# PSUM banks in a delta-rule attention: two for the pair steps, one for quantization and modulation

## The chip, the cores and the metric

The kernel runs on one core of a Trainium2 chip. Five engines work side by side, each through its own instructions in order: TensorE (PE, matmuls; its weight loads are listed as PEld), VectorE (DVE), ScalarE (ACT), GpSimd (POOL) and SyncE (SP, which here only issues DMAs). Matmul results land in PSUM, which has eight banks; ACT and DVE read them from there. The metric is the time of one execution on the device in microseconds (us), as the median of several runs.

## The reference

Two transformer blocks run one after the other on x of 2 batches, 1024 tokens and 512 channels. Each computes `x + ga * attn(norm(x) * (1 + ca) + sa)`, then the same with a feed-forward part and `sb, cb, gb`. The six vectors come from `silu(c) @ wmod`; this is called modulation. The two gates are kept away from zero: their magnitude is at least 0.25.

The attention of layer 0 is a gated delta rule with a state H of 64 x 64 per batch:

```
pred = q H;  surprise = sigmoid(sum((v - pred)^2))
H = a * H + (1 - a) * surprise * k^T (v - k H)
y = q H
```

k and q are normalized projections of the 512 channels to 64, v is a third projection and the decay a comes from a fourth through a sigmoid. y is normalized and projected back to 512.

The feed-forward part of layer 0 uses ternary weights. Each group of 64 weights has the mean of its magnitudes as a scale, and every weight becomes -1, 0 or 1 times that scale. The kernel does this quantization on the chip. Layer 1 has an RWKV attention and a feed-forward part with integer weights; the change doesn't touch it.

## The kernel before, in words

Tokens go in 16 chunks of 64 per batch, with both batches on the 128 partitions. Two chunks make a group, so that there are eight groups in layer 0's attention. For each group there are four kinds of work.

- `project(g)` normalizes two chunks, transposes them (`pt_a`), projects them (`pk`, `pv`) and leaves the scaled k and q in `kqr` (L385, L386).
- `pairs(g)` prepares all that doesn't need the state: products of each pair of steps in a chunk. It forms `kl` on DVE (L396), takes `pd` on PE, then six levels `pg` with decays multiplied in on DVE between them, then `pe`, `pm2`, `pse`, `pki` and `pik`, each a few small matmuls that are copied out by DVE or ACT before the next one. The last copy is `ik` (L475).
- `delta_chunk(c)` carries the state through one chunk. Its first DVE step is `wa` (L544), the new state is `h` (L518). It writes to the pool `ps_u`.
- `attention_out(g)` normalizes and projects y (`poa`) and adds it to x (`res_a` L229 on DVE, `xs` L230 on POOL).

Beside these, two other jobs fill the engines. `modulation(n)` loads a 512 x 512 slice of `wmod`, forms a row in `ps_...` (16 matmuls), copies it to `mrow_...` (L154, ACT), and turns it into columns (`pc_...`, read by DVE at L165) or a gate (`pg_ga`, `pg_gb`, read by ACT at L174 and by DVE at L176). `quantize(4)` calls `ternary` for four blocks of 128 x 512 weights: two ACT passes (`q_ab` L659, `q_sg` L661), one matmul that sums magnitudes (`pm_gu` L663), a copy out (`q_sc` L665, ACT), five DVE operations (L669 to L674) and a cast into the weight tile `wgu` (L675, ACT). There are 32 such blocks. The SBUF tiles of a block rotate through two buffers each.

`scan_all` writes the order of the program text. For g = 0 to 7: the two chunks of group g, `pairs(g + 2)`, `project(g + 3)`, `attention_out(g)`, one or two slices of modulation, and `quantize(4)`. (In the first round `pairs(1)` and `pairs(2)` both come here.) The text isn't the order on the engines. When the kernel is built, a planner puts the instructions of each engine in an order, from what it reckons to be ready and with work that stands earlier in the text first; it also hands out the buffers of each pool and adds the waits. That order is then fixed.

PSUM in layer 0's attention is dealt out by pools of whole banks: `ps_p` two (projection), `ps_g` one (pair steps), `ps_q` two (modulation and quantization), `ps_u` two (chunks) and `ps_o` one (output), eight in all. All tiles with the same tag share the buffers of that tag, and a tile gets a buffer when the earlier tile in it has been read for the last time. All names of `pairs` carry the tag `pg`. The pools are closed after the last group (`sp.close()`), and the feed-forward part opens `misc` (four banks, used first by the transposes `pt_f`, L202) and its own `ps_o` (four banks) in their place. Its SBUF tiles, `hh` and `hl` first, likewise take the place of the attention's; `good` (L712) is the last reduction of the attention.

The program holds the whole computation a second time with a step-by-step recurrence, behind a condition that is false for these inputs. The change edits its code too, but it isn't executed.

Of the kernel before, what the change touches and what calls it, by code (L numbers as in the profile page):

```python
# [8 lines left out]
F32 = mybir.dt.float32  # L9
# [5 lines left out]
PSUM = bass.MemoryType.PSUM  # L15

P = 128
B, S, D = 2, 1024, 512
ND = D // P
TT = 64  # L20

NC = S // TT
GT = 2
# [19 lines left out]
def block_pair_kernel(ctx: ExitStack, tc: tile.TileContext, a: dict, out: bass.AP):  # L43
    nc = tc.nc

    def pool(stack, name, bufs=1, **kw):
        return stack.enter_context(tc.tile_pool(name=name, bufs=bufs, **kw))
# [66 lines left out]
    def run(general, rs):  # L114
# [136 lines left out]
        with ExitStack() as la:  # L251
# [5 lines left out]
            sp = ExitStack()  # L257
# [1 line left out]

            ps_p = pool(sp, "ps_p", bufs=2, space=PSUM)  # L260
            ps_g = pool(sp, "ps_g", bufs=1, space=PSUM)
            ps_q = pool(sp, "ps_q", bufs=2, space=PSUM)
            ps_u = pool(sp, "ps_u", bufs=2, space=PSUM)
            ps_o = pool(sp, "ps_o", bufs=1, space=PSUM)
            proj = work = pool(sp, "proj", bufs=1)
# [35 lines left out]
            def both(to, weights, moving, start=True, stop=True, **kw):  # L301

                for b in range(B):
                    rows = slice(b * DS, (b + 1) * DS)
                    nc.tensor.matmul(  # L305
                        to[rows], weights[rows], moving[rows], start=start, stop=stop, **kw
                    )
# [81 lines left out]
            def pairs(g, kqr, al, v):  # L389

                gm = gms[g % 3]
                kqv = kqr.rearrange("p i (j t) -> p i j t", j=GT)
                gmv = gm.rearrange("p (j i) t -> p j i t", j=GT)
                kl = pair.tile([P, GT, TT], F32, tag="kl", name=f"kl_{g}", bufs=2)
                klf = kl.rearrange("p j t -> p (j t)")
                nc.vector.scalar_tensor_tensor(  # L396
                    klf, al, 1.0, kqr[:, 0], ALU.subtract, ALU.mult
                )

                pd = ps_g.tile([P, GT, TT], F32, tag="pg", name=f"pd_{g}")  # L400
                for j in range(GT):
                    both(pd[:, j], kl[:, j], kqv[:, 1, j])
                nc.vector.copy_predicated(
                    gmv[:, :, 2, :], mdiag.unsqueeze(1).to_broadcast([P, GT, TT]), pd
                )

                tot = al
                for h in LEVELS:  # L410
                    nb = TT // (2 * h)
                    ps = ps_g.tile([P, GT, 3, TT // 2], F32, tag="pg", name=f"pg_{g}_{h}")
                    right = kqr.rearrange("p i (n two h) -> p i n two h", two=2, h=h)[:, :, :, 1, :]
                    for j in range(GT):
                        both(
                            ps[:, j].rearrange("p i (n h) -> p i n h", h=h), kl[:, j],
                            right[:, :, j * nb:(j + 1) * nb, :],
                        )
                    nc.vector.copy_predicated(
                        gm.rearrange("p i (n two h) -> p i n two h", two=2, h=h)[:, :, :, 1, :],  # L420
                        masks[h].rearrange("p (n h) -> p n h", h=h).unsqueeze(1).to_broadcast(
                            [P, GT * 3, nb, h]
                        ),
                        ps.rearrange("p j i (n h) -> p (j i) n h", h=h),
                    )
                    tv = tot.rearrange("p (n two) -> p n two", two=2)
                    left = klf.rearrange("p (n two h) -> p n two h", two=2, h=h)[:, :, 0, :]
                    nc.vector.tensor_tensor(
                        left, left, tv[:, :, 1].unsqueeze(2).to_broadcast([P, GT * nb, h]), ALU.mult
                    )  # L430
                    nc.vector.tensor_tensor(
                        right, right,
                        tv[:, :, 0].unsqueeze(1).unsqueeze(3).to_broadcast([P, 3, GT * nb, h]),
                        ALU.mult,
                    )
                    nxt = pair.tile([P, GT * nb], F32, tag=f"tot{h}", name=f"tot_{g}_{h}")
                    nc.vector.tensor_tensor(nxt, tv[:, :, 0], tv[:, :, 1], ALU.mult)
                    tot = nxt
                atot = scan.tile([P, GT], F32, tag="atot", name=f"atot_{g}", bufs=3)
                nc.vector.tensor_copy(atot, tot)  # L440
                pe = ps_g.tile([P, GT, 3, TT], F32, tag="pg", name=f"pe_{g}")
                for j in range(GT):
                    both(pe[:, j, 0], kl[:, j], eye)
                    both(pe[:, j, 1], gmv[:, j, 0], eye)
                    both(pe[:, j, 2], kqv[:, 0, j], eye)

                kem = scan.tile([P, GT, 3, TT], F32, tag="kem", name=f"kem_{g}", bufs=3)
                nc.scalar.copy(kem, pe)

                im = pair.tile([P, GT, TT], F32, tag="im", name=f"im_{g}")  # L450
                nc.gpsimd.tensor_tensor(
                    im, gmv[:, :, 0], eye.unsqueeze(1).to_broadcast([P, GT, TT]), ALU.add
                )
                pm2 = ps_g.tile([P, GT, TT], F32, tag="pg", name=f"pm2_{g}")
                for j in range(GT):
                    both(pm2[:, j], gmv[:, j, 0], kem[:, j, 1])
                m2 = pair.tile([P, GT, TT], F32, tag="m2", name=f"m2_{g}")
                nc.scalar.copy(m2, pm2)
                pse = ps_g.tile([P, GT, TT], F32, tag="pg", name=f"pse_{g}")
                for j in range(GT):  # L460
                    both(pse[:, j], m2[:, j], im[:, j])
                inv = scan.tile([P, GT, TT], F32, tag="inv", name=f"inv_{g}", bufs=3)
                nc.vector.tensor_tensor(inv, pse, im, ALU.add)

                pki = ps_g.tile([P, GT, 2, TT], F32, tag="pg", name=f"pki_{g}")
                for j in range(GT):
                    both(pki[:, j, 0], kem[:, j, 2], inv[:, j])
                    both(pki[:, j, 1], inv[:, j], eye)
                ki = scan.tile([P, GT, 2, TT], F32, tag="ki", name=f"ki_{g}", bufs=3)
                nc.scalar.copy(ki, pki)  # L470
                pik = ps_g.tile([P, GT, TT], F32, tag="pg", name=f"pik_{g}")
                for j in range(GT):
                    both(pik[:, j], ki[:, j, 1], kem[:, j, 0])
                ik = scan.tile([P, GT, TT], F32, tag="ik", name=f"ik_{g}", bufs=3)
                nc.scalar.mul(ik, pik, 0.5)  # L475
                return gmv, kqv, kem, inv, atot, v, ki, ik
# [123 lines left out]
            def scan_all(chunk, p, name):  # L600
                h = p.tile([P, DS], F32, tag="h", name=f"h_init{name}")
                nc.vector.memset(h, 0.0)
                state[0] = h
                ops = [pairs(0, *project(0))]
                modulation(1)
                ahead = [project(1)]
                for g in range(NG):
                    yT = scan.tile([P, GT, TT], F32, tag="yT", name=f"yT_{g}{name}")
                    ysq = scan.tile([P, GT, TT], F32, tag="ysq", name=f"ysq_{g}{name}")
                    for j in range(GT):  # L610
                        chunk(GT * g + j, j, ops[g], yT, ysq)

                    for n in range(len(ops), min(g + 3, NG)):
                        ops.append(pairs(n, *ahead[n - 1]))
                        if n == g + 1:
                            attention_out(g, yT, ysq, f"{g}{name}")
                        for n in range(len(ahead) + 1, min(n + 2, NG)):
                            ahead.append(project(n))
                    if g:
                        attention_out(g, yT, ysq, f"{g}{name}")  # L620
                    modulation((1, 1, 1, 1, 1, 2, 1, 1)[g])
                    quantize(ND)
# [671 lines left out]
    with ExitStack() as rs:  # L1294
        bad = run(False, rs)
# [4 lines left out]
    with tc.If(odd != 0):  # L1300
        with ExitStack() as rs:
            run(True, rs)
# [46 lines left out]
```

## Time and profile before

| what | value |
|---|---|
| time, median of 3 runs | 1224.29 us (1224.22 to 1228.45) |
| the profiled execution: its time | 1233.09 us |
| its span, first to last instruction | 1231.2 us |
| granted TensorE clock, mean | 0.951 |
| PE busy | 1138.4 us (92%) |
| DVE busy | 730.3 us (59%) |
| ACT busy | 636.8 us (52%) |
| POOL busy | 410.4 us (33%) |

The profile is of one execution, so that its durations add up to its own span and not to the median. A row of the timeline gives the start in us from the start of the span, the duration in us, engine, line, operation, the tiles written and read, their shapes and the count; in brackets stands the idle time of the engine just before it and what ended that. Rows of the chain of work give start, duration and what ran. In the table of stretches each engine has its busy us and the number of its instructions; PEclk is the clock granted to TensorE. Matmuls are pipelined and their ends are modelled: a busy PE isn't PE at its peak.

### The profile page before, as it was taken

What the parts mean: (1) busy time and instruction counts of PE and PEld (TensorE: products, weight loads), DVE (VectorE), ACT (ScalarE), POOL (GpSimd) and SP (SyncE); (2) the same over time, 40 slices, a digit from 0 to 9 for tenths busy, and PEclk for the clock granted to TensorE, in tenths of its full rate; (3) what the DMA queues carried; (4) which work ended last, traced back from release to release, by engine and by line L of the source; (5) the groups of instructions that cost most, each with busy time, mean ns of one, the idle gap of its engine ahead of it and who ended that gap; (6) DMA issues with size and microseconds to landing.
All of it is one profiled execution on the core that took longest, in us unless ns stands there. A gap on an engine that the chain in (4) does not pass through costs nothing.

```text
span 1231.2 us, 17856 instructions
## 1 busy us (share of the span) xinstructions
PE 1138.4 (92%) x6746; PEld 854.5 (69%) x6746; DVE 730.3 (59%) x1509; ACT 636.8 (52%) x1423; POOL 410.4 (33%) x350
## 2 busy tenths in 40 slices
PE   5899999987999899999999979989899799999996
PEld 3667667554776688788788755737566488888884
DVE  3377677788777722622422789979899724242322
ACT  3367666567666533433433687876655644242421
POOL 1020112223444644644644313213212424242422
PEclk9899899876999999999999979979999899999998
DMA  8432121311110000000002311110000101010101
GB/s 204 113 87 71 35 89 62 127 54 35 52 43 26 1 1 1 1 1 1 1 35 69 95 35 35 52 35 1 1 1 10 43 26 35 1 35 1 35 1 38
DMA packets 40975, 48.72 MB, mean 40 GB/s; under 512 B 11568, under 2 KB 24880, under 8 KB 40880
## 3 DMA queue, kind: packets, MB, share of 16 engines
q1 hardware_dynamic: 39504, 45.92, 13.0%
q10 hardware_dynamic: 1376, 1.57, 0.4%
q8 instruction: 55, 0.90, 0.3%
q14 instruction: 40, 0.33, 0.1%
HBM read 43.28 MB, written 4.19 MB: 39 GB/s over the span
## 4 chain that ended last, share of the span: by engine, by line
PE 64%; DVE 21%; ACT 9%; issue 3%; POOL 2%; DMA 1%; SPq 1%; DVEq 0%; ACTq 0%
PE gu L762 14%; PE gui L1234 13%; PE pof L749 6%; PE poi L1214 6%; PE pow L1122 3%; PE pk L346 2%; PE pkvr L974 2%; DVE nd L1095 2%; PE u L305 2%; DVE q_m_p L671 2%; DVE xm L965 2%; PE pg L305 2%; PE poa L305 1%; PE pv L360 1%; DVE q_d_p L669 1%
## 5 line engine op out<-in xcount | busy, mean ns | idle before, releaser
L762 PE MATMUL gu<-hh,wgu 128*128 128x512 f32 x512 | 204.6, 402 | 4.9 <-DVE sg L771 3.5
L762 PE MATMUL gu<-hl,wgu 128*128 128x512 f32 x512 | 201.2, 395 | 4.0 <-DVE hl L221 2.7
L1234 PE MATMUL gui<-hp,wi 128*128 128x512 f32 x704 | 165.9, 390 | 0.0
L1234 PEld LDWEIGHTS gui<-hp,wi 128*128 128x128 f32 x704 | 131.8, 188 | 28.2 <-issue 0.8
L777 POOL TENSOR_TENSOR h0l<-sg,h0h 128x512 fp32r<-128x512 f32 x64 | 82.7, 1293 | 168.9 <-ACT h0h L775 168.9
L771 DVE TENSOR_TENSOR sg<-gu,sg 128x512 f32<-128x512 f32 x64 | 44.0, 687 | 139.9 <-ACT sg L770 136.6
L762 PEld LDWEIGHTS gu<-hh,wgu 128*128 128x128 f32 x512 | 97.3, 190 | 30.6 <-DVE sg L771 8.4
L762 PEld LDWEIGHTS gu<-hl,wgu 128*128 128x128 f32 x512 | 96.6, 189 | 27.1 <-DVE hl L221 4.5
L1249 POOL TENSOR_TENSOR h1l<-th,h1h 128x512 fp32r<-128x512 f32 x44 | 56.7, 1289 | 139.9 <-ACT h1h L1247 139.9
L1242 DVE SCALAR_TENSOR_TENSOR th<-th,gui 128x512 f32<-128x512 f32 x44 | 30.2, 687 | 121.7 <-ACT th L1241 121.7
L775 ACT CAST h0h<-sg 128x512 fp32r<-128x512 f32 x64 | 39.7, 621 | 86.8 <-DVE sg L773 84.9
L783 POOL TENSOR_TENSOR acc<-acc,hq 128x512 f32<-128x512 f32 x60 | 83.7, 1396 | 0.0
L1122 PE MATMUL pow<-w_wo,rw 128*64 128x512 f32 x256 | 73.5, 665 | 10.4 <-DVE rw L1113 10.0
L770 ACT ACTIVATE sg<-gu 128x512 f32<-128x512 f32 x64 | 38.1, 595 | 81.4 <-PE gu L762 81.4
L749 PE MATMUL pof<-wp,h0h 128*128 128x512 f32 x256 | 69.3, 392 | 1.7 <-ACT wp L675 1.7
L749 PE MATMUL pof<-wp,h0l 128*128 128x512 f32 x256 | 68.7, 389 | 0.0
L974 PE MATMUL pkvr<-xm,w_wk 128*128 128x256 f32 x256 | 62.1, 397 | 7.0 <-DVE xm L965 7.0
L1241 ACT ACTIVATE th<-gui,hsgate 128x512 f32<-128x512 f32 x44 | 30.3, 689 | 71.7 <-PE gui L1234 71.7
L1247 ACT CAST h1h<-th 128x512 fp32r<-128x512 f32 x44 | 27.3, 622 | 77.2 <-DVE th L1244 77.2
L974 PEld LDWEIGHTS pkvr<-xm,w_wk 128*128 128x128 f32 x256 | 48.3, 195 | 23.8 <-DVE xm L965 12.2
L974 PE MATMUL pkvr<-xm,w_wv 128*128 128x256 f32 x256 | 57.1, 380 | 1.0 <-DVE xm L965 1.0
L974 PE MATMUL pkvr<-xm,w_wr 128*128 128x256 f32 x256 | 56.6, 379 | 0.0
(368 smaller groups left out, 2497.6 us busy)
## 6 DMA issues: line engine op xcount, KB each, us to landing
wm<-in_wmod SPq DMA_DIRECT2D x22, 512.0 KB, 4.6
qst_gu<-in_wgu SPq DMA_DIRECT2D x32, 256.0 KB, 2.7
qst_p<-in_wp SPq DMA_DIRECT2D x16, 256.0 KB, 2.5
out<-oi SPq DMA_DIRECT2D x28, 128.0 KB, 2.4
xs<-in_x SPq DMA_DIRECT2D x2, 1536.0 KB, 15.8
kvt<-in_wq_gate SPq DMA_DIRECT2D x8, 256.0 KB, 2.6
kvt<-in_wq_up SPq DMA_DIRECT2D x8, 256.0 KB, 2.6
ist<-in_wq_down SPq DMA_DIRECT2D x7, 256.0 KB, 2.5
```

What stands on the lines that cost most here:

```text
L305: nc.tensor.matmul(to[rows], weights[rows], moving[rows], start=start, stop=stop, **kw)
L749: nc.tensor.matmul(pos[j], part[:, j * P:(j + 1) * P], wp[i // 4][:, i % 4, :], start=(i == 0 and z == 0), stop=(i == NH0 - 1 and z == 1),)
L762: nc.tensor.matmul(o, wgu[i // 4][:, d, s, (i % 4) * P:(i % 4 + 1) * P], part[:, d], start=(n == 0), stop=(n == 2 * ND - 1),)
L771: nc.vector.tensor_tensor(sg, gu[0], sg, ALU.mult)
L775: nc.scalar.copy(h1, h)
L777: nc.gpsimd.tensor_tensor(h2, h, h1.bitcast(F32), ALU.subtract)
L783: nc.gpsimd.tensor_tensor(acc, acc, hq, ALU.add)
L974: nc.tensor.matmul(ps[:, c * B:(c + 1) * B].rearrange("p b t -> p (b t)"), wkvr[i][:, d, (2 * z + c) * P:(2 * z + c + 1) * P], xm[d].rearr ...
L1122: nc.tensor.matmul(po[b * TT:(b + 1) * TT], rw[:, c, b, j * TT:(j + 1) * TT], wo1[:, c, :], start=(c == 0), stop=(c == ND - 1),)
L1214: nc.tensor.matmul(pos[j], part[:, j * P:(j + 1) * P], wdi[i // HS][:, i % HS, :], start=(i == 0 and z == 0), stop=(i == NH1 - 1 and z == ...
L1234: nc.tensor.matmul(o, wgi[i // HS][:, d, s, (i % HS) * P:(i % HS + 1) * P], part[:, d], start=(d == 0 and z == 0), stop=(d == ND - 1 and z ...
L1249: nc.gpsimd.tensor_tensor(h2, h, h1.bitcast(F32), ALU.subtract)
```

## The change

The pool `ps_q` gets one buffer in place of two, and the freed bank goes to `ps_g`: the tag of every PSUM tile in `pairs` becomes `pg0` for even groups and `pg1` for odd ones. The pool `ps_g` keeps `bufs=1`, now for two tags, so it holds two banks. The number of banks stays eight, and no instruction is added, removed or moved in the text. Of its seven tags three are shown; the other four (`pe`, `pm2`, `pse`, `pki`) change in the same way.

```diff
             ps_p = pool(sp, "ps_p", bufs=2, space=PSUM)
             ps_g = pool(sp, "ps_g", bufs=1, space=PSUM)
-            ps_q = pool(sp, "ps_q", bufs=2, space=PSUM)
+            ps_q = pool(sp, "ps_q", bufs=1, space=PSUM)
             ps_u = pool(sp, "ps_u", bufs=2, space=PSUM)
             ps_o = pool(sp, "ps_o", bufs=1, space=PSUM)
...
-                pd = ps_g.tile([P, GT, TT], F32, tag="pg", name=f"pd_{g}")
+                pd = ps_g.tile([P, GT, TT], F32, tag=f"pg{g % 2}", name=f"pd_{g}")
...
-                    ps = ps_g.tile([P, GT, 3, TT // 2], F32, tag="pg", name=f"pg_{g}_{h}")
+                    ps = ps_g.tile([P, GT, 3, TT // 2], F32, tag=f"pg{g % 2}", name=f"pg_{g}_{h}")
...
-                pik = ps_g.tile([P, GT, TT], F32, tag="pg", name=f"pik_{g}")
+                pik = ps_g.tile([P, GT, TT], F32, tag=f"pg{g % 2}", name=f"pik_{g}")
```

More of the change, by code (lines that the diff above doesn't have):

```diff
@@ L440, in pairs @@
                 nc.vector.tensor_copy(atot, tot)
-                pe = ps_g.tile([P, GT, 3, TT], F32, tag="pg", name=f"pe_{g}")
+                pe = ps_g.tile([P, GT, 3, TT], F32, tag=f"pg{g % 2}", name=f"pe_{g}")
                 for j in range(GT):
@@ L453, in pairs @@
                 )
-                pm2 = ps_g.tile([P, GT, TT], F32, tag="pg", name=f"pm2_{g}")
+                pm2 = ps_g.tile([P, GT, TT], F32, tag=f"pg{g % 2}", name=f"pm2_{g}")
                 for j in range(GT):
@@ L458, in pairs @@
                 nc.scalar.copy(m2, pm2)
-                pse = ps_g.tile([P, GT, TT], F32, tag="pg", name=f"pse_{g}")
+                pse = ps_g.tile([P, GT, TT], F32, tag=f"pg{g % 2}", name=f"pse_{g}")
                 for j in range(GT):
@@ L463, in pairs @@
                 nc.vector.tensor_tensor(inv, pse, im, ALU.add)
-                pki = ps_g.tile([P, GT, 2, TT], F32, tag="pg", name=f"pki_{g}")
+                pki = ps_g.tile([P, GT, 2, TT], F32, tag=f"pg{g % 2}", name=f"pki_{g}")
                 for j in range(GT):
```

## The prediction

> **What bounds the kernel now.** I began with the busy row of the page, then the table of busy time by stretch, because the diff touches only the attention of layer 0, which runs from about 40 to 300 us.
>
> ```profile
> core 0: us, PE busy (x) PEld busy (x) DVE busy (x) ACT busy (x) POOL busy (x), PEclk, DMA share, GB/s
> 40.00:220.00 180.00, 174.12 (x2111) 122.97 (x2110) 125.17 (x439) 112.05 (x345) 30.91 (x34) 0.92 0.23 69
> 220.00:300.00 80.00, 66.79 (x663) 38.60 (x662) 67.92 (x196) 50.64 (x155) 17.97 (x16) 0.78 0.21 67
> 300.00:405.00 105.00, 97.44 (x404) 72.26 (x404) 76.72 (x117) 67.64 (x124) 48.44 (x34) 0.97 0.14 41
> ```
>
> The reader is to see two stages. Up to 220 us TensorE (PE) is the fullest, though its ends are modelled; from 220 to 300 VectorE (DVE) works 67.92 of 80 us and has 12.1 us idle. The feed-forward part behind it is untouched: what the attention gains or loses arrives at the end one to one.
>
> Next I asked the chain of work that ended last how the attention hands over to the feed-forward part. Its last steps are all quantization on DVE, then hh, then the first gate/up matmul:
>
> ```profile
> 294.75 1.41 DVE q_m_gu L673
> 296.16 0.60 DVE q_d_gu L669
> 296.76 0.34 DVE q_m_gu L674
> 297.10 0.34 DVE q_m_gu L671
> ...
> 298.12 0.32 DVE q_d_gu L672
> 298.45 0.34 DVE q_m_gu L673
> 298.97 0.63 ACT hh L219
> ```
>
> So the end of this part is set by the last of 32 weight blocks that `ternary` quantizes (call them b0 to b31, four behind each group) and not by the recurrence, whose last state h (L518) is there at 285.05.
>
> Then I took each tile's own view and wrote down when it starts. **Two serial lines** come out. The pair steps of the eight groups stand end to end on the one bank of `ps_g`: pd starts at 40.6, 60.7, 94.1, 115.0, 147.3, 174.9, 202.8, 228.8, and ik (L475), the last reader, at 60.3, 93.6, 114.3, 144.4, 173.8, 202.4, 228.5, 256.5. The other line is `ps_q`, which takes modulation and quantization in the order of the program text: the first pm of a four starts when the modulation's matmuls end, and the next modulation right behind the fourth pm.
>
> **Part 1, a second bank for pair steps.** Nothing is added: same matmuls, copies and DMAs; only who waits for whom. Inside a group a second bank can't help, since all seven kinds of tile of a group carry the same tag. Between groups, pd need no longer wait for ik of the group before. How much did it wait for that alone? pd also needs kl (L396). In the timeline around group 7:
>
> ```profile
> 228.07 0.28 DVE L396 SCALAR_TENSOR_TENSOR kl<-al,kqr 128x128 f32<-128x128 f32 x1
> ...
> 228.47 0.28 ACT L475 ACTIVATE ik<-pik 128x128 f32<-128x128 f32 x1 [0.28 <-PE pik L305]
> ...
> 228.80 0.69 PE L305 MATMUL pd<-kqr,kl 64*64 64x64 f32 x8 [0.37 <-ACT ik L475]
> ```
>
> kl uses no PSUM, its inputs were there at 218.7 (end of L386), and still it ran at 228.07: DVE first did blocks b16 to b18 and the residual of the group before, which stand earlier in the text. So the bank held pd by 228.80 - 228.35 = 0.45 us, not by the ten that ik against kqr suggests. The same difference, pd's start less kl's end, gives 4.5 (group 1), 1.2, 2.7, 0.8, 0.8, 1.5, 0.45 us. In groups 4 and 5 ik was already done when kl ended, so these are no waits for the bank: 10.3 us in all. Who would be early? The chunk of group 3 reads its pair steps (wa, L544) at 173.4, though they were ready at 144.7; from group 2 on such slack is 17 to 29 us, except the last group with 12. Group 1 has hardly any: its ik ends at 93.9, its first wa is at 95.2. Bounds: 0 to -10.3 us. I take -2.0 (groups 6 and 7, 1.5 + 0.45), since these free DVE in the stage that decides.
>
> Here the Trainium skill ("Perfetto Trace Analysis", section "Optimizing Tensor Performance") speaks against half of the change: independent matmul groups should rotate through different PSUM banks, so that emptying one overlaps the next group's matmuls. By that rule part 1 is worth its 10.3 us and part 2 costs about as much, sum zero; by the rows part 1 is worth 2.0, because kl and not the bank comes last.
>
> **Part 2, one bank for quantization and modulation.** Again no instruction is added. Three waits are new.
>
> (a) The first pm of a four waited for mrow to be copied out of the other bank's tile; now it waits until the modulation's second tile (pc or pg) is read by DVE. Around the last gate, in the timeline:
>
> ```profile
> 278.76 1.12 PE L171 MATMUL pg_gb<-mrow_gb,pick 128*128 128x512 f32 x2
> 279.72 0.38 PE L663 MATMUL pm_gu<-q_ab_gu,bones_h 128*128 128x512 bf16 x1
> 282.53 0.69 DVE L176 TENSOR_SCALAR gb<-pg_gb 128x512 f32<-128x512 f32 x1
> ```
>
> pm at 279.72 would have to wait for 283.2, 3.5 us. But the pm's user on DVE was late too: q_d (L669) of b28 ran at 283.1. With pm 0.4, copy q_sc (L665) 0.6 and some 0.1 of hand-over, q_d could start 1.1 us after the release, at 284.3: 1.2 late. Worked out so for each four: b0 0.3, b4 0, b8 0, b12 1.0, b16 1.1 (pc_ca is read at 221.1, pm was at 215.0), b20 1.2, b24 0.1, b28 1.2. And ps_sb, which followed ps_ga in the other bank at 238.2, has to wait for L176 of ga, 241.0: 2.8. Together 7.7.
>
> (b) The next modulation's first matmul waits for the fourth q_sc to end, not only for its pm to be issued: 0.5, 0, 0.2, 0, 0.7, 0.8, 0.7: 2.9 us.
>
> (c) The second pm of a couple waits for the first's q_sc: up to 0.8 us (b7: 136.9 for 136.1), but b7's q_d came at 143.0, so 0.
>
> If nothing absorbs it, 7.7 + 2.9 = 10.6 us. What stands behind these waits: pm and ps wait on PE, whose queue runs in order, so the u and py matmuls of the recurrence stand behind a pm that was placed too early; q_d to q_m (five DVE operations, 2.2 us a block) and the cast to wgu (L675) wait for it. Bounds: above, 10.6; below, -2: while a block waits DVE is free for the chunks, which it served late (wa at 256.2 with inputs from 245.5). Of the 10.6, 2.0 fall before 190 us (b0, b12 and 0.5 + 0.2), where DVE has 30% idle and the line has gaps to regain it (137.4 to 141.9 before ps_gb); I count them nothing. The other 8.6 fall in the stage whose last item is b31. DVE's idle 12.1 us covers them only if it lies where the blocks wait; the chain says the opposite, so I count them full.
>
> **Part 3, the hand-over.** The feed-forward part's first tiles take the place of the attention's PSUM pools. pt_f (L202, 16 transposes, 3.67 us) started at 294.52, right after the last q_sc ended (294.47): the feed-forward part's first pool lies over banks of `ps_p`, `ps_g` and, by this tie, `ps_q`. With `ps_q` down to one bank behind the pair steps' two, the tie may be gone and pt_f may run earlier. It gains little: hh starts at 298.97, 0.1 us behind `good` (L712, 298.70 to 298.86), the last reader of memory that hh takes over; ht was done at 298.22. Cover gone, 0.7 us. ht also needs the two `qst` slots, so b31's q_sg (ends 292.8). Bounds: 0 to -5.5 (hh at 293.5 if DVE took L712 early); I take 0, the row nearest, since L712 stands behind b31's operations on DVE.
>
> **Sum.** -2.0 + 8.6 + 0 = +6.6 us. The profiled execution took 1233.09 us (span 1231.2), 8.8 above the median 1224.29 of the runs; the difference lies outside what I change, so 1224.3 + 6.6 = 1230.9, say **1231 us**.
>
> One thing the rows can't give: the order on every engine is set when the kernel is built, from the waits that the planner foresees. New waits give a new order in all 260 us of this part; 2.5% of them is 6 us. This widens the range both ways.
>
> **Rivals.** About 0.5% (6 us) is what a measurement of this kernel can tell from no change.
> *Hidden, 35%*: the stage from 220 to 300 us is held by the sum of DVE's work, which is unchanged; blocks and chunks change places in its 12.1 us of idle time. For it: kl, wa and q_d all wait for a busy DVE. Against it: DVE's groups in this stretch show 2.7 us of idle time before res_a and 3.6 before h, which no block fills. It gives 8.6 x (1 - 67.92/80) = +1.3, 1225.6 us.
> *Faster, 20%*: the pair line is what counts. Group 1's steps come 4.5 us earlier and move the first wa of its chunk, which has only 1.3 us slack; with groups 6 and 7 (2.0) and the hand-over (0.7) that is -7.2, 1217 us. It decides from the point at which kl of group 7 stands before 224 us, that is, when pairs of two groups really overlap by over 4 us in each of the last groups.
> *Slower, 45%*, own range +6.2 to +18: the sum above; at its upper end the line of `ps_q` falls behind by two blocks, which cost 9.8 us at the pace of b28 to b31 (279.7 to 299.3, four blocks), 8.6 + 9.8 = 18.4.
>
> The likeliest gives the predicted time. The range takes in the faster case's -7.2 and a little of its tail, to 1215 (-9), and the slower case up to 1242 (+18); left out are about 1 in 10 on each side. Chances: faster 0.20, same 0.35, slower 0.45.
>
> **What would show it.** Right: the first pm of a four starts behind L165 or L176 and not before; DVE's idle time between 220 and 300 us grows from 12.1; hh stands near 305 in place of 298.97; the rows after it keep their durations. Part 1 right: pd of groups 4 to 7 still starts within 1 us of kl's end. Wrong: hh before 296, or kl of the last group some 10 us before ik of the one before it (then the planner did use the second bank and my reading of DVE's order was of an order that the bank itself had caused); or a change in the rows behind 300 us.

## The result, and the profile after

The changed kernel takes **1243.54 us** (median of 4 runs, 1242.33 to 1244.12) against 1224.88 us for the kernel before on the same chip: ratio **1.0137, 95% interval 1.0116 to 1.0157**. It is slower, as forecast, but by 18.7 us (16.8 by the ratio) and not by 6.6, and the median lies 1.5 us beyond the range. Measured once more, on another chip (run a0_after below), it took 1240.10 us, 13.6 us above the kernel before there. So the size of the loss is known to some 5 us only. Its profiled execution took 1243.14 us (span 1241.3).

The table of busy time by stretch of the changed kernel, with the columns of the one shown before (stretch and its length, then busy us and number of instructions of PE, PEld, DVE, ACT and POOL, granted clock, DMA share, GB/s):

```profile
40.00:220.00 180.00, 172.21 (x2030) 119.98 (x2028) 121.05 (x418) 108.91 (x331) 29.46 (x32) 0.91 0.21 60
220.00:300.00 80.00, 67.43 (x729) 41.51 (x727) 66.28 (x197) 48.32 (x159) 14.76 (x14) 0.82 0.27 83
300.00:405.00 105.00, 95.01 (x382) 68.61 (x381) 78.82 (x125) 67.48 (x124) 46.12 (x33) 0.94 0.14 41
```

In the stage that the prediction watched, 220 to 300 us, DVE's idle time grew from 12.1 to 13.7 us only. The loss is in the stage ahead of it: between 40 and 220 us DVE has done 121.05 us of work, where it had done 125.17.

The end of the attention in the timeline of the changed kernel (start, duration, engine, line, operation, tiles, shapes; in brackets the idle time just before and its releaser):

```profile
302.95 0.41 DVE L673 TENSOR_TENSOR q_m_gu<-q_m_gu,q_sg_gu 128x512 bf16<-128x512 bf16 x1
304.03 0.41 DVE L674 TENSOR_TENSOR q_m_gu<-q_d_gu,q_m_gu 128x512 bf16<-128x512 bf16 x1
...
306.03 0.15 DVE L712 TENSOR_REDUCE good<-miss 128x1 f32<-128x16 f32 x1
306.30 1.14 ACT L219 CAST hh<-ht_f 128x512 fp32r<-128x512 f32 x2 [0.45 <-DVE good L712]
```

It has the form of before: the last blocks on DVE, `good`, then hh, at 306.30 in place of 298.97. The hand-over to the second bank, around group 7 in the same timeline:

```profile
234.92 0.27 ACT L475 ACTIVATE ik<-pik 128x128 f32<-128x128 f32 x1
...
237.61 0.28 DVE L396 SCALAR_TENSOR_TENSOR kl<-al,kqr 128x128 f32<-128x128 f32 x1
...
239.65 0.64 PE L305 MATMUL pd<-kqr,kl 64*64 64x64 f32 x8
```

The pair steps of group 6 were over 4.5 us before pd of group 7 started, so the second bank brought nothing here. The last gate, and the hand-over of PSUM:

```profile
289.72 0.68 DVE L176 TENSOR_SCALAR gb<-pg_gb 128x512 f32<-128x512 f32 x1
291.01 0.61 PE L663 MATMUL pm_gu<-q_ab_gu,bones_h 128*128 128x512 bf16 x1
292.99 0.69 DVE L669 SCALAR_TENSOR_TENSOR q_d_gu<-q_sc_gu,q_ab_gu 128x512 bf16<-128x512 bf16 x1
```

```profile
264.11 0.28 ACT L475 ACTIVATE ik<-pik 128x128 f32<-128x128 f32 x1
264.44 0.90 PE L202 MATMUL pt_f<-ident,xn_f 128*128 128x128 f32 x3 [0.48 <-ACT ik L475]
```

pm stands behind L176, as the one bank demands. The transposes pt_f now start right behind ik, the last reader of the pair steps' bank, 30 us earlier than before; hh gains nothing from it, since it still waits for `good`.

### The profile page after: what moved, and what is told of

Same layout as the page of the kernel before. It is cut to its first block, busy times and chain, and to the rows that moved or that the text cites. A ratio compares the mean times of both kernels' runs of the same rounds, so it can differ in the third digit from the quotient of the medians.

```text
span 1241.3 us, 17853 instructions
## 1 busy us (share of the span) xinstructions
PE 1144.1 (92%) x6746; PEld 858.7 (69%) x6746; DVE 732.6 (59%) x1509; ACT 637.2 (51%) x1423; POOL 408.5 (33%) x350
## 4 chain that ended last, share of the span: by engine, by line
PE 44%; DVE 17%; ACT 8%; issue 2%; POOL 1%; DMA 0%; DVEq 0%; ACTq 0%; POOLq 0%
PE gu L762 14%; PE gui L1234 13%; PE pof L749 7%; PE poi L1214 6%; DVE nd L1095 2%; PE pow L1122 2%; DVE xm L965 2%; DVE q_m_p L671 1%; DVE m L1066 1%; DVE q_d_p L669 1%; DVE nd L1104 1%; POOL xs L230 1%; DVE nd L1111 1%; PE pkvr L974 1%; ACT sv L1087 1%
## 5 line engine op out<-in xcount | busy, mean ns | idle before, releaser
L749 PEld LDWEIGHTS pof<-wp,h0h 128*128 128x128 f32 x256 | 48.8, 192 | 11.9 <-ACT wp L675 1.8
```

The costliest lines, as they stand in the source:

```text
L749: nc.tensor.matmul(pos[j], part[:, j * P:(j + 1) * P], wp[i // 4][:, i % 4, :], start=(i == 0 and z == 0), stop=(i == NH0 - 1 and z == 1),)
```

## Where the time comes from

A second profile of the kernel before (run e0_before below, 1225.43 us, near the median; here called the typical one) differs from the recorded one (1233.09 us), though DVE, ACT and POOL do the same instructions in the same order. Its hh starts earlier:

```profile
292.04 0.62 ACT L219 CAST hh<-ht_f 128x512 fp32r<-128x512 f32 x1 [0.76 <-DVE mv_f L186]
```

So there are two comparisons. Against the recorded profile (298.97), hh of the changed kernel comes 7.3 us later. Against the typical one it comes 14.3 us later, and the span ends 17.8 us later (1241.3 to 1223.5). The other 3.5 us belong to that execution or its chip and not to the change. In the second profile of the changed kernel (a0_after) hh starts at 306.35 and the span ends 931.7 us behind it; in the two profiles of before it ends 931.5 and 932.2 us behind hh, and in the recorded one of the changed kernel 935.1. So behind hh nothing is gained or lost, as the prediction had it.

The tiles' starts say where the lag begins. In round 1 of the loop, the modulation group of `cb0` and block b4 in the kernel before (recorded profile), then in the changed one, there with the ACT pass that makes b4's input ready:

```profile
114.51 0.58 ACT L154 COPY mrow_cb<-ps_cb 128x512 f32<-128x512 f32 x1
115.96 0.95 PE L161 MATMUL pc_cb<-pick,mrow_cb 128*128 128x2 f32 x8
116.78 0.38 PE L663 MATMUL pm_gu<-q_ab_gu,bones_h 128*128 128x512 bf16 x1
```

```profile
110.07 0.63 ACT L659 ACTIVATE q_ab_gu<-qst_gu 128x512 bf16<-128x512 f32 x1
...
117.45 0.60 ACT L154 COPY mrow_cb<-ps_cb 128x512 f32<-128x512 f32 x1
126.53 1.05 PE L161 MATMUL pc_cb<-pick,mrow_cb 128*128 128x2 f32 x8
129.03 0.16 DVE L165 TENSOR_SCALAR cb<-pc_cb 128x8 f32<-128x8 f32 x1
135.24 1.97 PE L305 MATMUL poa<-early,yT 64*64 64x512 f32 x2
137.13 0.61 PE L663 MATMUL pm_gu<-q_ab_gu,bones_h 128*128 128x512 bf16 x1
```

mrow is 3 us late, pc 10.6, and b4's pm 20.4. b4's input is there at 110.7 and the bank is free at 129.2, but pm stands in PE's queue behind pe, pr and poa of other groups. PE waits for nothing there. In its list of waits (total us, times, longest us) the releases of `ps_q` make up 1.0 us in the whole attention:

```profile
PE pm_gu L663 <- ACT q_sc_gu L665: 0.7, 1, 0.7
PE pm_gu L663 <- DVE sb L165: 0.3, 1, 0.3
```

So what PE lost isn't time spent waiting for the bank. What differs is the order of the instructions: the planner, which reckons with the new waits, has put other work ahead of pm. Between 120 and 140 us PE is full in all three profiles. Their tables by stretch, first the changed one, then the recorded one of before, then the typical one:

```profile
120.00:140.00 20.00, 20.00 (x183) 14.21 (x181) 8.46 (x32) 7.30 (x24) 3.51 (x4) 0.70 0.08 26
140.00:160.00 20.00, 18.29 (x198) 11.88 (x196) 14.86 (x44) 14.28 (x42) 2.40 (x2) 0.79 0.17 52
```

```profile
120.00:140.00 20.00, 20.00 (x180) 12.76 (x180) 11.00 (x34) 9.76 (x28) 3.74 (x4) 0.74 0.12 39
```

```profile
40.00:220.00 180.00, 172.59 (x2165) 122.75 (x2161) 130.81 (x452) 112.15 (x346) 34.86 (x36) 0.95 0.23 67
120.00:140.00 20.00, 20.00 (x231) 13.69 (x231) 15.02 (x44) 14.07 (x40) 5.01 (x5) 1.00 0.09 28
```

Two things differ: how much DVE work PE's order feeds (8.46, 11.00, 15.02 us), and the granted clock (0.70, 0.74, 1.00). Over 40 to 220 us the changed kernel does 9.8 us less DVE work than the typical one before. At the pace of the stage behind (66.28 of 80 us) that is 11.8 of the 14.3 us. In blocks: by 220 us 16 scales q_sc are out, against 19 in the typical profile and 18 in the recorded one; three blocks at the 4.9 us that the prediction used are 14.7. These are estimates of one and the same loss and don't add up, and a lower clock is one way for DVE's work to come late. The experiments ask what made this: the waits for the bank, the second pair bank, the order, or the clock.

## The experiments

All ratios are to the kernel before on the same chip, with 95% intervals; every kernel computes the whole. Times of runs on different chips are compared by their ratios. The letter and digit at the head of a run's name are used as its short name.

**Each half of the change alone.** First the kernel before again, then part 2 alone (the pair steps keep one bank, the eighth bank lies idle):

```diff
-            ps_q = pool(sp, "ps_q", bufs=2, space=PSUM)
+            ps_q = pool(sp, "ps_q", bufs=1, space=PSUM)
```

> The kernel before once more. The profiled execution took 1233.09 us, 8.8 above the median of its timed runs. If that was one execution's own delay, this profile takes 1223 to 1229 us and hh starts 5 us or more earlier than 298.97; if profiles of it are always slower, it takes 1231 us or more again. Timed against itself: ratio within 0.3% of 1.

Measured 1225.55 us (1219.89 to 1231.71), 0.9999 (0.9971 to 1.0027). The delay of the recorded profile was that one execution's own.

> The kernel before with only part 2 of the change: ps_q has one bank, the pair steps keep their single one, and the eighth bank stays unused. Theory A (sharing one bank between modulation and quantization costs the time, the second bank of the pair steps is worth about nothing): as slow as the changed kernel, 1238 to 1248 us, and the first pm of the second four (b4) comes more than 10 us later than the 116.8 us of before. Theory B (the second bank lets the planner put pair steps early and pushes the blocks back): within 6 us of before, 1219 to 1231 us, b4 near 117 us.

Measured 1235.78 us, **1.0070 (1.0044 to 1.0097)**, +8.6 us by the ratio: the size that the prediction took for part 2, and between the two theories of the expectation. b4's pm comes at 122.61, 5.8 us late where theory A asked for 10. PE's list of waits shows the bank more than in the changed kernel, but still only 3.6 us in the four largest rows that name it (its longest wait, 5.3 us in six times, is of pm for its input q_ab):

```profile
PE ps_gb L149 <- ACT q_sc_gu L665: 2.0, 1, 2.0
PE pm_gu L663 <- ACT q_sc_gu L665: 0.9, 2, 0.7
PE ps_ga L149 <- ACT q_sc_gu L665: 0.4, 1, 0.4
PE ps_cb L149 <- ACT q_sc_gu L665: 0.3, 1, 0.3
```

Next, the two streams apart: the same two banks as before, but one for quantization and one for all of modulation; then only modulation's second tile (pc, pg) in the other bank.

```diff
-            ps_q = pool(sp, "ps_q", bufs=2, space=PSUM)
+            ps_q = pool(sp, "ps_q", bufs=1, space=PSUM)
+            ps_m = pool(sp, "ps_m", bufs=1, space=PSUM)
...
-                rows = mod_rows(load_wmod(layer, i, nc.sync), ps_q, "q", sc, key, w0a)
+                rows = mod_rows(load_wmod(layer, i, nc.sync), ps_m, "m", sc, key, w0a)
...
-                        mods[key] = mod_gate(rows, ps_q, "q", key, to)
+                        mods[key] = mod_gate(rows, ps_m, "m", key, to)
```

The change of `mod_rows` is in e2_split only; `mod_gate` and `mod_cols` take `ps_m` in both.

> Pair steps on one bank, quantization on one bank, modulation on a bank of its own (eight banks). Theory A in the form that modulation and quantization hinder each other in one bank: 1219 to 1229 us, near or below before, since no block waits for a modulation tile any more. If instead the blocks need two banks for themselves (the second pm of a couple waiting for the first copy), it stays slow, 1236 us or more. Theory B says nothing against before: 1219 to 1231 us.

> As the run with only part 2, but the modulation's second tile (pc or pg) is put in the eighth bank; its rows (ps) and the blocks' pm share the one bank of ps_q. This takes away my wait (a) alone and leaves (b) and (c). If (a) is the cause (my sum: 7.7 of 10.6 us): back to 1221 to 1231 us. If the loss comes from the rows' tile or from couples of pm sharing a bank: 1236 us or more.

e2_split: 1222.04 us, **0.9977 (0.9960 to 0.9993)**, slightly faster than before. e3_second: 1231.10 us, 1.0038 (1.0019 to 1.0058): with wait (a) of the prediction taken away, about half of e1's loss is gone. In e2_split hh starts at 288.66; its table by stretch:

```profile
40.00:220.00 180.00, 174.14 (x2154) 122.70 (x2152) 131.77 (x450) 114.64 (x349) 32.94 (x36) 0.95 0.25 75
```

In these four DVE's work done by 220 us goes with hh: 131.77 us and 288.7, 130.81 and 292.0, 125.17 and 299.0, 121.05 and 306.3. Over all twenty profiles the tie is looser (correlation -0.70; p1 below has 129.13 us and hh at 304.4).

**The second pair bank.** Here modulation goes to the projection's two banks, so that quantization is alone in its one (the call of `mod_cols` changes likewise); with one bank for the pair steps, one bank of the eight lying idle (f1), then two (f2):

```diff
-                rows = mod_rows(load_wmod(layer, i, nc.sync), ps_q, "q", sc, key, w0a)
+                rows = mod_rows(load_wmod(layer, i, nc.sync), ps_p, "pp", sc, key, w0a)
...
-                    mods[key] = mod_gate(rows, ps_q, "q", key, to)
+                    mods[key] = mod_gate(rows, ps_p, "pp", key, to)
```

> All modulation tiles go to the projection's pool (tag pp, two banks), quantization has the one bank of ps_q, the pair steps one bank (seven banks in use). Base for the next run. Theory C: blocks no longer stand behind modulation, so faster than the run with only part 2 unless the projection suffers: 1222 to 1234 us.

> The same with two banks for the pair steps: this is part 1 of the change alone, without modulation and quantization sharing a bank. Theory A (the second bank is worth nothing, since kl and not the bank comes last): within 4 us of the run with one. Theory B (the second bank puts pair steps early and costs time in itself): 6 us or more slower. If the bank bound the pair steps: 5 us or more faster.

> The changed kernel once more, on the chip of these runs. The runs with only part 2 gave +0.7% and the change as a whole +1.4% on another chip. If the parts add so, 1240 to 1246 us here, some 8 us above part 2 alone; if that was a difference of chips, 1233 to 1239 us.

f1 1233.50 us, 1.0062 (1.0039 to 1.0086); f2 1242.17 us, 1.0127 (1.0084 to 1.0169); the changed kernel again, 1240.10 us, 1.0112 (1.0076 to 1.0148). The second bank cost 8.7 us here, and 4 to 8 on top of e1 (1240.10 and 1243.54 against 1235.78; by the ratios 5 to 8): the parts add. Only group 1 overlaps by much in the changed kernel: its pd starts at 57.91, and ik of group 0 ends at 61.67. So the second bank was given to group 1 alone (k2), or kept from it, with groups 0 and 1 in one bank and the alternation from group 2 on (k1):

```diff
-                pd = ps_g.tile([P, GT, TT], F32, tag=f"pg{g % 2}", name=f"pd_{g}")
+                pd = ps_g.tile([P, GT, TT], F32, tag=f"pg{int(g == 1)}", name=f"pd_{g}")
```

```diff
-                pd = ps_g.tile([P, GT, TT], F32, tag=f"pg{g % 2}", name=f"pd_{g}")
+                pd = ps_g.tile([P, GT, TT], F32, tag=f"pg{max(g - 1, 0) % 2}", name=f"pd_{g}")
```

The first is k2, the second k1; the other six tags of `pairs` likewise.

> The changed kernel, but only group 1's pair steps use the second bank; all other groups share the first. Part 2 is in it as before. Group 1 is the one whose pair steps really overlap another group's in the changed kernel (pd at 57.9, ik of group 0 at 61.4). Theory E (the second bank's 8 us come from that early overlap, which reorders all behind it): as slow as the changed kernel, 1238 us or more. Theory F (the cost comes from the later groups): as the run with only part 2, 1231 to 1237 us.

> The changed kernel, but groups 0 and 1 share the first bank, and the alternation starts with group 2. Theory E: as the run with only part 2, 1231 to 1237 us. Theory F: 1238 us or more. If both this and the run before are near 1235, the two overlaps cost only together; if both are near 1241, any second bank costs the same.

k2 1234.92 us, 1.0096 (1.0068 to 1.0125); k1 1230.54 us, 1.0028 (1.0008 to 1.0047). k1 looks like theory E: without group 1's overlap most of the loss is gone. k2 speaks against it: with group 1's overlap alone the time should have been that of the changed kernel, and it falls where theory F put it. And k1, with a second bank, is faster than e1, which has none. So no group can be named as the cost. The next runs ask whether it is the order.

**The order.** One line of the program text is moved, pools and tags stay (each such order of the calls is called a text below): modulation ahead of a round's pair steps (h1 to h3, r1; the first diff), or behind quantization (p1, p2, r2; the second).

```diff
+                    modulation((1, 1, 1, 1, 1, 2, 1, 1)[g])
                     for n in range(len(ops), min(g + 3, NG)):
...
-                    modulation((1, 1, 1, 1, 1, 2, 1, 1)[g])
                     quantize(ND)
```

```diff
-                    modulation((1, 1, 1, 1, 1, 2, 1, 1)[g])
                     quantize(ND)
+                    modulation((1, 1, 1, 1, 1, 2, 1, 1)[g])
```

> The changed kernel with the call of modulation moved in the text from behind the pair steps, projection and output of a round to in front of them; pools, tiles and waits are those of the changed kernel. Theory C (the loss comes from the order that the planner makes: the modulation's tiles come late, and the blocks behind them in the one bank come later still): b4 before 120 us and 1224 to 1234 us. Theory D (the loss is the waits for the bank themselves, as I summed them): no better than the changed kernel, 1238 us or more.

> The kernel before with only the call of modulation moved in the text ahead of a round's pair steps, as in the run on the changed kernel; banks as before. If the order of the modulation is what matters everywhere: faster than before, 1215 to 1223 us. If it mattered only because one bank made the blocks stand behind it: within 4 us of before, 1222 to 1230 us.

> Modulation and quantization on a bank each (which gave -0.23%), and the call of modulation moved forward. With its own bank the modulation holds up no block, so its place should matter little: 1217 to 1226 us; a version that beats both kernels if it stays below 1222.

> The changed kernel with the two last lines of a round exchanged: the four blocks of a round are written ahead of the round's modulation group. Pools, tags and waits are those of the changed kernel. Order theory: the late modulation group of round 1 no longer stands ahead of blocks b4 to b7, so b4's scale matmul starts before 125 (137.1), hh before 300 (306.3) and the median is 1224 to 1234. One-bank theory (the bank's waits cost what the order doesn't): each four still follows a group through the one bank, so hh stays at 303 or later and the median at 1237 to 1246. Clock theory: hh follows the half-clock time: with less than 7 us of it in 65-220 hh is before 299, with 17 us or more after 303, wherever the group stands.

> The version with a bank for modulation and a bank for quantization (all pair steps in one bank, which was 0.9977 of the time before) with the same two lines exchanged. There the two streams don't meet in a bank, so the order of the two calls only moves the planner's choices. If order is luck, the result lies anywhere within 1 per cent of it: 1216 to 1234. If quantization ahead of modulation is better in itself, it is 1212 to 1221, and p1 beats the changed kernel by 8 us or more as well.

> One bank for modulation and quantization, all pair steps in one bank, and the modulation call written ahead of a round's pair steps: the partner of the changed kernel with modulation first (1230.26, 1.0021), without the second pair bank. If the second pair bank costs something in itself, in every written order, as it did twice (1235.78 to 1243.54 in the text's own order; 1233.50 to 1242.17 with modulation in the projection's banks), this one is 5 to 9 us faster than its partner: 1221 to 1226. If the cost was the draw of the planner's order, the pair of orders may fall either way: 1226 to 1238, and in a mean over the three texts the second bank is worth nothing either way.

> The same with quantization written ahead of modulation: the partner of the changed kernel with quantization first (1238.70, 1.0066), without the second pair bank. Second bank costly in itself: 1230 to 1234. Draw of the order: 1233 to 1245, either side of its partner. Over the three texts with one bank for both, the mean of the pairs-in-one-bank kernels then says what sharing alone costs; the prediction took 8.6 us for it, so a mean of 1233 to 1236 bears that out.

The measured ratios, by the banks and by the text:

| banks | text as it was | modulation first | quantization first | mean |
|---|---|---|---|---|
| two for both streams, pairs one (before) | 1 | 1.0020 | not run | 1.0010 |
| one each, pairs one (e2) | 0.9977 | 1.0034 | 0.9964 | 0.9992 |
| one for both, pairs one (e1) | 1.0070 | 1.0091 | 0.9986 | 1.0049 |
| one for both, pairs two (changed) | 1.0137, 1.0112 | 1.0021 | 1.0066 | 1.0071 |

The intervals reach 0.0013 to 0.0036 to either side; the last row's mean takes its first entry as 1.0125. Moving the one line in the changed kernel brings 9.8 us back on the same chip (a0 1240.10, h1 1230.26 us; b4's pm at 118.76), with every pool, tag and instruction kept: that much of its loss comes with the order, whatever clock came with it included. And the second pair bank costs 0.55%, gains 0.70% and costs 0.80% in the three texts: mean +0.22%, or 3 us, with an error of about 0.46%. With f1 and f2 as a fourth pair (+0.65%) it is +0.33% with an error of 0.35%. **So its cost in one text can't be told from a draw of the order** (a small cost of its own isn't excluded, since three of the four pairs show one). Within a row the standard deviation is 0.46% (seven degrees of freedom), or 5.6 us. Sharing shows at the edge of this noise: the six kernels with one bank for both streams have a mean of 1.0060, the five with two banks for them 0.9999. That is 0.61% or 7.5 us, with an error of 0.28% or 3.4 us, and its 95% interval just takes in zero. (e3, which is in between, and the runs k, f and n are left out of these means, and what a text costs in itself isn't taken out of the scatter.)

Of the expectations, h1 came out as theory C had it, and h2 (1228.41 us) as the case in which the place of the modulation matters only with one bank. h3 missed: 1230.56 us, where a place of no account would have given 1217 to 1226. p2 (1223.65 us) lies where luck of the order put it and not where quantization first is better in itself.

p1 also shows that the late group of round 1 isn't the whole story. Its b4 comes early, right behind the modulation's read:

```profile
110.85 0.17 DVE L165 TENSOR_SCALAR sb<-pc_sb 128x8 f32<-128x8 f32 x1 [0.93 <-PE pc_sb L161]
111.22 0.39 PE L663 MATMUL pm_gu<-q_ab_gu,bones_h 128*128 128x512 bf16 x1
```

Between 116 and 220 us its clock is full, and still hh starts at 304.4 (1238.70 us). Here hh doesn't wait for `good`, which ends at 301.7, but for the last gate, whose matmuls now follow the last block through the one bank:

```profile
303.60 0.69 DVE L177 SCALAR_TENSOR_TENSOR gb<-gb,mag_gb 128x512 f32<-128x512 f32 x1
304.40 1.14 ACT L219 CAST hh<-ht_f 128x512 fp32r<-128x512 f32 x2 [1.12 <-DVE gb L177]
```

So the move isn't quite neutral: it gives the attention another last item, worth up to 2.7 us here. Of the theories in its expectation, order had b4 right and hh wrong, the half-clock time (13.7 us) fell between the two cases of the clock, and the outcome was that of the one bank. r1 (1239.07 us) refutes a second bank that costs 5 to 9 us in every text; r2 (1225.53 us) landed better than either theory had it.

**The clock.** 24 unread matmuls should hold the clock up where the changed kernel's falls; n2 puts them into the kernel before.

```diff
+                    for z in range(2 if g in (2, 3) else 0):
+                        nc.tensor.matmul(
+                            raw[:, 256 + z % 2 * P:256 + z % 2 * P + P], bones_h, bones_h,
+                            start=True, stop=True, skip_group_check=True,
+                        )
```

> The changed kernel with 24 more matmuls that nobody reads: in groups 2 and 3, behind the four matmuls of each of the six levels, two of bones_h by bones_h (128x128 bf16) into the columns of the level's bank that the level leaves free. Nothing of the result changes. In both profiles of the changed kernel TensorE ran at half clock for 17.1 us from 128.1 and for 3.4 us from 148.5, with TensorE busy in all of 120-140. Clock as the cause: if the added matmuls keep the clock up there, the mean granted clock of 120-140 is 0.95 or more (0.70 before), the fifth block's scale matmul comes before 128 (137.1), hh before 299 (306.3), and the median is 1226 to 1233 (ratio 1.000 to 1.006). Order as the cause, clock a mere companion: hh stays at 304 or later and the median at 1238 to 1246 whatever the clock of 120-140. If the clock stays at half there although the matmuls are there, the run says nothing of the cause, only that they don't hold it.

> The same 24 unread matmuls in the kernel before: the price of adding them where the clock is typically not halved in 65-176. They are 24 by at most 0.2 us, 5 us at most of an engine that is full in that stretch, and they move the planner's order. Clock theory: no stretch to cure, so 1224 to 1231, not faster than before by more than 2 us. Rival: if the kernel before gains more than 3 us from them too, then its runs are commonly held back by a half-clock stretch as well, and the changed kernel's is not special.

n1 1251.75 us (1238.68 to 1253.94), 1.0156 (1.0089 to 1.0224); n2 1238.07 us, 1.0078 (1.0052 to 1.0104). One such matmul takes 0.23 us, 5.5 us for all. n1's table by stretch:

```profile
120.00:140.00 20.00, 19.53 (x184) 14.26 (x183) 8.44 (x30) 7.28 (x22) 3.45 (x4) 0.72 0.15 53
140.00:160.00 20.00, 19.28 (x161) 11.30 (x163) 13.55 (x37) 11.76 (x29) 1.38 (x1) 0.60 0.13 38
```

They didn't hold the clock: by its own terms n1 says nothing of the cause. n1's four runs lie 15 us apart, so that its size isn't settled either. n2's cost, 9.6 us by the ratio, is beyond what was expected and beyond the matmuls' own 5.5 us; that a new order made the rest was not tested.

## Why the prediction was wrong in size

- **What bounds the kernel.** The end was read rightly: quantization on DVE, `good`, hh, and behind hh one to one. The stage was not. The sum weighed each wait by what it does from 220 us on; the lag is there before, and the 80 us behind only carry it on.
- **The step that failed** is the order of the instructions. The text named it ("New waits give a new order in all 260 us of this part") and let it widen the range only; in the sum it was put at nothing, and each wait was reckoned as a delay within the order of before. It shows in two terms:
  - In part 1: "Bounds: 0 to -10.3 us. I take -2.0". In this text the second bank cost 4 to 8 us on top of e1, and 8.7 from f1 to f2, outside these bounds. Since part 2 alone measured what it was taken for, nearly all of the miss stands here.
  - In part 2: "of the 10.6, 2.0 fall before 190 us [...] where DVE has 30% idle and the line has gaps to regain it; I count them nothing". b4's own delay came out of the rows as 0; in the trace its pm is 20.4 us late, though PE waited 1.0 us for `ps_q` in all. Between 120 and 140 us PE is busy for 20.00 of 20 us and DVE for 8.46, so DVE's idle time was no reserve there: it went with the work that PE hadn't handed over yet, and hh comes 14.3 us later than in the typical profile.
- **Part 1, the reading.** That kl, not the bank, comes last held: in groups 4 to 6 pd starts 0.57 to 0.75 us behind kl's end (1.8 in group 7), and only groups 1 and 6 start before their forerunner's ik has ended, by 3.8 and 0.9 us. Over the texts the term isn't measured well enough to know its sign. The Trainium skill's rule of rotating banks ("Perfetto Trace Analysis", section "Optimizing Tensor Performance") had 8.6 us in its favour in one text, and 7 and 10 us against it in the two others.
- **Part 2, the size.** 8.6 us taken, 8.6 measured in e1 (5.4 to 11.9), 8.7 from h2 to r1 with modulation first, 7.5 (error 3.4) in the mean over texts. With quantization first r2 is no slower than before in its own text. So the number held as far as it can be measured, but not by the way that was summed: in e1 PE waits some 4 us for the bank, and in the changed kernel 1.0. That is luck in part.
- **Part 3.** Right: the tie to `ps_q` is gone, pt_f is early, hh waits for `good`.
- **"The difference lies outside what I change"**, said of the 8.8 us between the profiled execution and the median, was wrong: 6.9 us lie ahead of hh, 4.7 of them between 117 and 141 us, in the stage that changes. The hh forecast, near 305 for 298.97, was met (306.30) because both of these executions have the same half-clock time between 60 and 220 us (last section); from the typical 292.04, hh moved by twice as much.
- **The size of "the order".** "2.5% of them is 6 us" was a guess without a row behind it; that the scatter over the texts is 5.6 us is luck. The changed kernel lies about 0.5% above the mean of its row, one such deviation. The mean of the row is 1.0071, 8.7 us.
- **The rivals.** The upper end of "slower" (18.4 us, two blocks behind) names a real loss, three blocks in fact, but it is lost from round 1 on and not at the end; that 18.4 is near 18.7 is luck. "Hidden" fell in this text. "Faster" had its first step right: group 1's ik comes at 84.63 for 93.62 and its first wa at 88.75 for 95.18. By group 2 the lead is gone (ik at 115.21 for 114.33), and kl of group 7 stands at 237.6, not before 224.

## What to carry over

Where a planner writes the order from the waits it foresees, a change of a PSUM pool is also a new draw of the order: here some 0.5% to either side. Before a pool is called good or bad, move one line that leaves pools and instructions alone and measure again, compare means over a few texts, and look whether the stage still ends with the same item (in p1 it didn't). A bank for each of two streams that otherwise take turns in one beat both kernels in two texts of three: e2_split, and with quantization written first 1223.65 us, 0.9964 (0.9948 to 0.9980). With modulation first it was slower than before (h3, 1.0034), so it is no sure gain either: its mean, 0.9992, can't be told from the 1.0010 of before.

## What the runs showed of the hardware

The granted clock isn't the same in two executions of one program. In all twenty profiles it is 1.0 or 0.5, in stretches of 3.4 us and multiples of it. Between 60 and 220 us the recorded profile of before has 20.5 us at half clock (10.2 of them from 128.5), the typical one 7.0. Since DVE does the same instructions in the same order in both, their starts can be compared one by one, ahead of that stretch of 10.2 us and behind it; first the typical profile, then the recorded one:

```profile
116.81 0.28 DVE L518 SCALAR_TENSOR_TENSOR h<-h,atot,u 128x64 f32<-128x64 f32 x1 [0.34 <-PE u L305]
...
133.75 0.75 DVE L229 SCALAR_TENSOR_TENSOR res_a<-poa,rs_y,ga 128x512 f32<-128x512 f32 x1 [0.24 <-PE poa L305]
```

```profile
119.08 0.28 DVE L518 SCALAR_TENSOR_TENSOR h<-h,atot,u 128x64 f32<-128x64 f32 x1 [0.34 <-PE u L305]
...
140.67 0.75 DVE L229 SCALAR_TENSOR_TENSOR res_a<-poa,rs_y,ga 128x512 f32<-128x512 f32 x1 [1.63 <-PE poa L305]
```

The recorded one is 2.3 us behind ahead of the stretch and 6.9 us behind it, as it still is at hh. So 10.2 us at half clock, while PE was full, cost 4.7 us; the other 2.3 are older than 65 us. The order is the same, and nothing but the clock was found to differ there: in this pair the clock is taken for the cause.

Both profiles of the changed kernel have 20.5 us at half clock between 60 and 220 us, 17.1 of them from 128.1 and 3.4 from 148.5. Eight matmuls of one form, at 125.88 and at 130.27, on either side of that edge:

```profile
125.88 0.55 PE L305 MATMUL pg<-kqr,kl 64*64 64x96 f32 x8
...
130.27 0.91 PE L305 MATMUL pg<-kqr,kl 64*64 64x96 f32 x8
```

By the same share, the 13.5 us more than in the typical profile are worth about 6 us: an estimate from the 4.7 for 10.2. So some half of the 14.3 us between the typical profiles may be the clock's, and the rest the order's; the 7.3 us between the two profiles with equal half-clock time fit this. Over all twenty profiles half-clock time in this stretch and the start of hh go together (correlation 0.81, without n1 0.69), but not closely: p2 has 17.1 us of it and hh at 293.3, r1 10.8 us and hh at 303.2. Whether the changed order brought the clock down isn't shown. The Trainium skill ("TensorE: Matmul & The Clock Gate", "Part 1: The HAM clock gate") says that a monitor sets the array's clock by how busy it has been of late. These runs don't bear that out in what the profile counts as busy: PE is busy for all 20 us from 120 to 140 at a mean clock of 0.70, and 24 matmuls of 128x128 didn't hold it. Whether a version that holds the clock would bring these microseconds back stays open.
